# A four-layer convolution stack: transfers of layer 1 tied to its matmuls, layer 2's normalisation ahead of one copy of its column sums

## Chip, cores and metric

The kernel runs on one core of a Trainium2 chip, written in Bass and Tile. The metric is the device time of one execution in microseconds (us). Everything is float32.

## The reference

The input is x, four images of 16 channels of 512 x 512. Four layers each normalise their input in groups of two channels, apply a convolution and add the result to the input. Layers 1 and 2 are the ones concerned here.

```python
# layer 0: two blocks of three dilated 5x5 convolutions over neighbouring channels, tanh
x = x + L0(_gn(x))
# layer 1: quantise, 3x3 convolution of 16 to 16 channels, scale back
x_q = round(clip(x_cl / scale_input, -n, n))          # x_cl is _gn(x), scale_input from its largest magnitude
acc = conv(x_q, w_hwio, padding=1)
x = x + acc * (scale_input * scale_weight) + bias
# layer 2: a mean over 17 columns and then 17 rows, per channel
x = x + conv(conv(_gn(x), kx), ky)
# layer 3: a 3x3 complex convolution of the spectrum (rfftn, irfftn)
x = x + L3(_gn(x))
```

## The kernel before

The layers run one after the other, each from a tensor in HBM to the next (x1, x2, x3). `run` calls `layer0`, `layer1`, `layer2` and `layer3`. In the inner loops of all layers the order of the work is written out by hand (`tc.manual_schedule()`): each engine does its instructions in the order of the program text, and the SP engine (SyncE) issues loads and stores in that order too. A load that waits for its buffer holds up whatever SP has behind it.

**Layer 1** (`layer1`, lines 825 to 973) walks over 64 chunks of eight image rows; all four images are in a chunk together, each on its own 32 partitions (two rows by 16 channels). For chunk u:

- `load(u)` brings four transfers of 256 KB, one for each image b, from x1 into a tile `l1x` (line 890). The pool of these tiles has four buffers. Line 883 loads the row ahead of the first chunk, line 892 the last row.
- `rounded(u)` normalises and rounds it on ScalarE (ACT, line 900) and VectorE (DVE, lines 901 and 902) into one of three `l1q` tiles.
- `products(u)` issues 256 matmuls of 32 x 32 x 512 (line 915) into one of two PSUM tiles `l1p`: eight groups (n, which is a tap row a and a column shift d) by four images b by four output row pairs j. Each has a weight load of its own. The groups with d < 3 read `l1q`; the last two, d = 3, read the unrounded `l1x` and add the input.
- `write(u)` scales the result on ACT (line 929) into a tile `l1o` of three buffers, takes its statistics on DVE (line 931), and SP stores it in four transfers of 256 KB to x2 (line 933).

The order in one turn of the loop is load(u+2), products(u), rounded(u+1), write(u-1). After the loop, line 955 aggregates the statistics, and a chain of small operations gives layer 2's normalisation.

**Layer 0** already has the device that the change brings to layer 1: its `products` keeps the last matmul of each group in `marks`, and its `load` (line 200) makes a transfer wait for one of them by `add_manual_dep`, so many bytes to a mark.

**Layer 2** (`layer2`, lines 976 to 1092) walks over 64 images of one channel, i. `load(i)` (line 1011) brings 1 MB; `normal(i)` (line 1017) normalises on ACT into `l2n`; `first(i)` does the first pass, 32 matmuls with the band matrix (helper `box`, line 999), four ACT copies from PSUM into `l2y` (line 1028); `second(i)` does the second pass, 32 matmuls, and adds the input on DVE (line 1039), takes statistics (line 1040) and stores 1 MB to x3 (line 1041); `column_sums(i)` multiplies the result by three column vectors (line 1051), copies the sums on ACT into `l2s` (line 1056) and stores them on SP (line 1058). The product of each quarter hb of the image's rows leaves three rows of PSUM at partitions 32 hb to 32 hb + 2, and there is one ACT copy for each. Layer 3's edge products read these sums from HBM.

The order in one turn is load(i+3), first(i+1), column_sums(i-1), second(i), normal(i+2).

Of the kernel before, what the change touches and what calls it, by code (L numbers as in the profile page):

```python
# [744 lines left out]
class Kernel:  # L745
# [79 lines left out]
    def layer1(self, x1, x2, gn):  # L825
        tc, nc = self.tc, self.nc
        scale, bias, amax = gn
        with ExitStack() as ctx:
            wpool = ctx.enter_context(tc.tile_pool(name="l1w", bufs=1))
            xin = ctx.enter_context(tc.tile_pool(name="l1x", bufs=4))  # L830
            work = ctx.enter_context(tc.tile_pool(name="l1work", bufs=2))

            wrep = self.load(wpool, "l1_w")
# [38 lines left out]
            qs = [wpool.tile([P, 4, W + 2], F32, name=f"l1q_{i}") for i in range(3)]  # L872
            for q in qs:
                nc.vector.memset(q, 0.0)
            raws = {}

            def load(u):

                x = raws[u] = xin.tile([P, 4, W], F32, name=f"l1x_{u}", tag="x")
                if u < 0:  # L880
                    nc.vector.memset(x[:, 3], 0.0)
                    for b in range(B):
                        nc.sync.dma_start(x[32 * b + C : 32 * b + 32, 3], x1[b, 0])
                    return
                whole = 4 if u + 1 < NYB else 3
                if whole == 3:
                    nc.vector.memset(x[:, 3], 0.0)
                for b in range(B):
                    rows = x1[b, 8 * u + 1 : 8 * u + 1 + 2 * whole].rearrange("(k y) c w -> (y c) k w", y=2)
                    nc.sync.dma_start(x[32 * b : 32 * b + 32, 0:whole], rows)  # L890
                    if whole == 3:
                        nc.sync.dma_start(x[32 * b : 32 * b + C, 3], x1[b, H - 1])

            def rounded(u):
                lo = 3 if u < 0 else 0
# [11 lines left out]

            def products(u):
                ps = psum.tile([P, B, W], F32, name=f"l1p_{u}", tag="ps")
                for n, (a, d) in enumerate((a, d) for d in range(4) for a in range(2)):  # L910
                    for b in range(B):
                        for j in range(4):
                            v, k = (u - 1, 3) if a + j == 0 else (u, a + j - 1)
                            rows = slice(32 * b, 32 * b + 32)
                            nc.tensor.matmul(  # L915
                                ps[32 * j : 32 * j + 32, b, :],
                                wt[rows, a, d],
                                qs[v % 3][rows, k, d : d + W] if d < 3 else raws[v][rows, k],
                                start=(n == 0),
                                stop=(n == 7),  # L920
                                skip_group_check=True,
                            )
                raws.pop(u - 1)
                return ps

            def write(u, ps):
                o = work.tile([P, B, W], F32, name=f"l1o_{u}", tag="o", bufs=3)
                for k in range(0, B, 2):
                    nc.scalar.activation(o[:, k : k + 2], ps[:, k : k + 2], AF.Identity, bias=wbi, scale=osc)
                for b in range(B):  # L930
                    nc.vector.bn_stats(st[b][:, u, :], o[:, b, :])
                    dst = x2[b].rearrange("h c w -> (h c) w")
                    nc.sync.dma_start(dst[u * P : (u + 1) * P, :], o[:, b, :])

            with tc.tile_pool(name="l1ps", bufs=2, space=PSUM) as psum, tc.manual_schedule():
                for u in range(-1, 2):
                    load(u)
                for u in range(-1, 1):
                    rounded(u)
                last = None  # L940
                for u in range(NYB):
                    if u + 2 < NYB:
                        load(u + 2)
                    ps = products(u)
                    if u + 1 < NYB:
                        rounded(u + 1)
                    if last is not None:
                        write(u - 1, last)
                    last = ps
                write(NYB - 1, last)  # L950

            gps = ctx.enter_context(tc.tile_pool(name="l1gps", bufs=2, space=PSUM))
            mv = wpool.tile([P, B, 2], F32, name="l1mv")
# [22 lines left out]
    def layer2(self, x2, x3, sums, gn, l3):  # L976
        tc, nc = self.tc, self.nc
        res, under_way = [], []
        with ExitStack() as ctx:
# [3 lines left out]
            edge = ctx.enter_context(tc.tile_pool(name="l2edge", bufs=1))  # L983
            ps1 = ctx.enter_context(tc.tile_pool(name="l2p1", bufs=2, space=PSUM))
            ps2 = ctx.enter_context(tc.tile_pool(name="l2p2", bufs=2, space=PSUM))
            ps3 = ctx.enter_context(tc.tile_pool(name="l2p3", bufs=1, space=PSUM))
            gps = ctx.enter_context(tc.tile_pool(name="l2gps", bufs=1, space=PSUM))
            eps = [ctx.enter_context(tc.tile_pool(name=f"l2e{n}", bufs=1, space=PSUM)) for n in "us"]
            band = self.load(wpool, "c_band")
            cs = self.load(wpool, "c_cs")  # L990
            mv = wpool.tile([P, B, G, 2], F32, name="mv3")
# [21 lines left out]
            def normal(i):  # L1013
                b, c = divmod(i, C)
                g = c // 2
                xns[i] = work.tile([P, 4, W], F32, name=f"l2n_{i}", tag="xn")
                nc.scalar.activation(  # L1017
                    xns[i], xts[i], AF.Identity, bias=gn[b][1][:, g : g + 1], scale=gn[b][0][:, g : g + 1]
                )
# [25 lines left out]
            def column_sums(i):  # L1045

                b, c = divmod(i, C)
                o = outs.pop(i)
                pc = ps3.tile([P, W], F32, name=f"l2p3_{i}", tag="pc")
                for hb in range(4):  # L1050
                    nc.tensor.matmul(  # L1051
                        pc[32 * hb : 32 * hb + 3], cs[:, hb, :], o[:, hb, :], start=True, stop=True, skip_group_check=True
                    )
                so = work.tile([P, W], F32, name=f"l2s_{i}", tag="so")
                for hb in range(4):
                    nc.scalar.copy(so[32 * hb : 32 * hb + 3], pc[32 * hb : 32 * hb + 3])  # L1056
                for t in range(3):
                    nc.sync.dma_start(sums[b][t, c], so[t : t + 97 : 32])

# [9 lines left out]
            with tc.manual_schedule():  # L1069
                for i in range(3):  # L1070
                    load(i)
                normal(0)
                first(0)
                normal(1)
                for i in range(n + 1):
                    if i + 3 < n:
                        load(i + 3)
                    if i + 1 < n:
                        first(i + 1)
                    if i > 0:  # L1080
                        column_sums(i - 1)
                    if i < n:
                        second(i)
                    if i + 2 < n:
                        normal(i + 2)
                    advance()
                    if i > 0 and i % C == 0:
                        b = i // C - 1
                        res.append(self.group_stats(gps, self.stats, f"x3_{b}", mv[:, b], G))
                        if b == 1:  # L1090
                            under_way.append(self.edges(l3, 0, res, sums, tiles, *eps))
# [536 lines left out]
```

## Time and profile before

| what | value |
|---|---|
| median of three runs | 5569.73 us (5559.56 to 5571.75) |
| the profiled execution | 5572.08 us, its span 5570.3 us |
| granted TensorE clock | 0.978 |
| layer 1, first to last matmul's start (L915) | 3216.8 to 3860.2 us |
| layer 2, first pass to last column sum's start (L999, L1051) | 3890.5 to 4554.6 us |
| TensorE busy / DVE / ACT | 92% / 73% / 47% of the span |

The span runs from the first to the last instruction of the profiled execution. PE is TensorE's matmuls, PEld its weight loads, which overlap with them. A group of the page is read as: line, engine, operation, out<-in, partitions x elements, xcount | busy us, mean ns of one | idle time just before them, and what ended most of it; "issue" there is idle time in which the engine waited for nothing that the profile shows. A row of the timeline is read as: start in us, duration in us, engine, line, operation, tiles, xcount, and in brackets the idle time ahead of it and what ended it. A row of the windows gives a stretch, its length, the busy time of each engine with its instructions, the granted clock, the mean busy share of the 16 DMA engines and what they moved in GB/s.

### The profile page before, as it was taken

The page shows a single profiled execution, that of the slowest core. Times are in us where ns is not written, and L with a number is a line of the kernel's source. Part 1 is how long each engine was busy: PE and PEld are TensorE (multiplying, and loading weights), DVE is VectorE, ACT ScalarE, POOL GpSimd, SP SyncE. Part 2 cuts the span into 40 slices and gives each one's busy share as a digit, 9 for nine tenths or more (in the row PEclk, how much of TensorE's full clock was granted, in tenths as well). Part 3 has the DMA queues.
Part 4 walks back from the last instruction along what each step waited for, and adds up shares of the span by engine and source line. Part 5 has one row for each costly group of instructions (what it writes and reads, how often), then busy time and mean ns, then how long its engine had stood idle before and what let it go on. Part 6 is the DMA issues. An engine that isn't in the chain of part 4 may idle for free.

```text
span 5570.3 us, 267073 instructions
## 1 busy us (share of the span) xinstructions
PE 5105.7 (92%) x125040; PEld 3556.9 (64%) x125040; DVE 4044.1 (73%) x4738; ACT 2611.6 (47%) x4143; POOL 6.1 (0%) x18
## 2 busy tenths in 40 slices
PE   3999999999999989989999788887999979999999
PEld 2665665666675656666666545554887866777776
DVE  7766889657987659897678854445555568888887
ACT  2533335433345523443122444443665656666665
POOL 0000000000000000000000000000000000000000
PEclk9999999999999999999999999998999999999999
DMA  5555545565445555544454377876565655555554
GB/s 192 136 147 129 153 139 153 142 150 137 122 151 160 142 131 143 150 124 118 89 132 126 117 198 209 214 209 191 199 214 192 214 176 137 143 145 149 148 144 119
DMA packets 373827, 860.92 MB, mean 155 GB/s; under 512 B 52209, under 2 KB 74353, under 8 KB 356081
## 3 DMA queue, kind: packets, MB, share of 16 engines
q1 hardware_dynamic: 317072, 694.76, 44.1%
q10 hardware_dynamic: 55648, 149.08, 9.4%
q8 instruction: 979, 16.04, 1.3%
q14 instruction: 128, 1.04, 0.1%
HBM read 503.74 MB, written 339.90 MB: 151 GB/s over the span
## 4 chain that ended last, share of the span: by engine, by line
PE 84%; issue 5%; ACT 4%; DVE 4%; DMA 2%; SPq 1%; ACTq 0%; DVEq 0%
PE m L499 50%; PE l1p L915 10%; PE l2p L999 5%; PE u L1464 4%; PE s L1405 4%; PE u L1405 4%; PE u L1427 2%; PE pt L1439 2%; ACT l2n L1017 2%; ACT l2s L1056 2%; PE l2p L1051 1%; SPq L200 1%; DVE frame L415 1%; DMA frame<-y 0%; PE pr L1449 0%
## 5 line engine op out<-in xcount | busy, mean ns | idle before, releaser
L499 PE MATMUL m<-frame,l0w 32*32 32x512 f32 x86016 | 2920.8, 608 | 257.1 <-issue 151.7
L499 PEld LDWEIGHTS m<-frame,l0w 32*32 32x32 f32 x86016 | 1968.4, 104 | 1208.6 <-issue 604.0
L415 DVE SCALAR_TENSOR_TENSOR frame<-frame,frame 128x2376 f32<-128x2376 f32 x232 | 606.6, 2625 | 4.7 <-PE m L499 0.4
L915 PE MATMUL l1p<-l1q,l_wt 32*32 32x512 f32 x12288 | 489.2, 603 | 109.6 <-issue 68.1
L915 PEld LDWEIGHTS l1p<-l1q,l_wt 32*32 32x32 f32 x12288 | 274.4, 103 | 266.0 <-issue 186.0
L1039 DVE TENSOR_TENSOR l2o<-l2x,l2p 128x512 f32<-128x512 f32 x256 | 172.6, 674 | 283.1 <-PE l2p L999 283.1
L617 ACT ACTIVATE junk<-xb,neg 128x1024 f32<-128x1024 f32 x256 | 294.1, 1149 | 80.1 <-DVE top L601 38.2
L532 ACT COPY C<-m 128x1024 f32<-128x1024 f32 x64 | 61.6, 1014 | 537.2 <-PE m L499 408.7
L999 PE MATMUL l2p<-k_c_band,l2n 128*128 128x144 f32 (+1 forms) x2048 | 275.1, 295 | 36.5 <-DMA l2x<-x 15.5
L999 PEld LDWEIGHTS l2p<-k_c_band,l2y 128*128 128x128 f32 x2048 | 256.8, 190 | 75.0 <-issue 54.3
L999 PEld LDWEIGHTS l2p<-k_c_band,l2n 128*128 128x128 f32 x2048 | 262.2, 197 | 48.6 <-ACT l2n L1017 41.4
L999 PE MATMUL l2p<-k_c_band,l2y 128*128 128x144 f32 (+1 forms) x2048 | 284.3, 292 | 6.0
L901 DVE TENSOR_SCALAR l1t<-l1t 128x2048 f32<-128x2048 f32 x64 | 78.5, 1226 | 271.2 <-ACT l1t L900 271.2
L900 ACT ACTIVATE l1t<-l1x,l1own,l1own 128x1024 f32<-128x1024 f32 x128 | 151.8, 1233 | 237.4 <-DMA l1x<-x 234.6
L1464 PE MATMUL u<-k_c_hil,zt 128*128 128x128 f32 x2048 | 256.0, 279 | 0.0
L384 DVE STREAM_TRANSPOSE frame<-xp 128x1056 f32<-128x1056 f32 x128 | 161.6, 1278 | 127.0 <-ACT xp L358 127.0
L1464 PEld LDWEIGHTS u<-k_c_hil,zt 128*128 128x128 f32 x2048 | 238.5, 192 | 2.1 <-issue 0.8
L1440 ACT COPY zt<-pt 128x512 f32<-128x512 f32 x256 | 131.5, 601 | 210.3 <-PE pt L1439 210.3
L1028 ACT COPY l2y<-l2p 128x512 f32<-128x512 f32 x256 | 149.7, 585 | 169.1 <-PE l2p L999 169.1
L1370 DVE TENSOR_TENSOR xc<-l3n,k_c_tab 128x2048 f32<-128x2048 f32 x64 | 146.7, 2292 | 109.6 <-ACT l3n L1354 109.6
L915 PE MATMUL l1p<-l1x,l_wt 32*32 32x512 f32 x4088 | 213.3, 632 | 0.0
L1483 DVE SCALAR_TENSOR_TENSOR l3o<-u,l3t 128x256 f32<-128x256 f32 x512 | 192.8, 430 | 23.4 <-ACT l3t L1475 21.0
(302 smaller groups left out, 6553.0 us busy)
## 6 DMA issues: line engine op xcount, KB each, us to landing
y<-y ACTq DMA_DIRECT2D x128, 528.0 KB
frame<-y SPq DMA_DIRECT2D x512, 132.0 KB
xb<-in_x SPq DMA_DIRECT2D x128, 512.0 KB
x<-xb ACTq DMA_DIRECT2D x128, 512.0 KB
x<-l1o SPq DMA_DIRECT2D x256, 256.0 KB
l2x<-x SPq DMA_DIRECT2D x64, 1024.0 KB
x<-l2o SPq DMA_DIRECT2D x64, 1024.0 KB
l3x<-x SPq DMA_DIRECT2D x256, 256.0 KB
```

Source lines behind the costliest of these rows:

```text
L384: nc.vector.transpose(v[:, :, 4 + h : 68 : 2], xp)
L415: self.nc.vector.scalar_tensor_tensor(o, x, f, y, ALU.mult, ALU.add)
L499: ins = nc.tensor.matmul(ps[PX * j : PX * j + PX, i, :].rearrange("p (k r) -> p k r", r=64), w[rows, n], v[rows, k0 : k0 + 8, r0 : r0 + 64 ...
L617: nc.scalar.activation(junk, xs[h], f, bias=neg, accum_out=self.out_sums[n][:, 2 * t + h : 2 * t + h + 1])
L900: nc.scalar.activation(t[:, at], x[:, at], AF.Identity, bias=own[1], scale=own[0])
L915: nc.tensor.matmul(ps[32 * j : 32 * j + 32, b, :], wt[rows, a, d], qs[v % 3][rows, k, d : d + W] if d < 3 else raws[v][rows, k], start=(n ...
L999: nc.tensor.matmul(ps[:, lo:hi], lhs[:, k, at : at + P], band[:, j : j + hi - lo], start=(k == 0), stop=(k == 3), skip_group_check=True,)
L1028: nc.scalar.copy(yts[i][:, wb, :], ps)
L1039: nc.vector.tensor_add(o[:, hb, :], xt[:, hb, :], ps)
L1405: nc.tensor.matmul(ps[b][32 * j : 32 * j + 32], f[rows, n, j, :], x[rows, j, :], start=(i == 0), stop=(i == 2 and tag == "s"), skip_group_ ...
L1464: nc.tensor.matmul(po[:, bass.ts(k, P)], zt[:, b, k ^ 1, :], hil[:, k, :], start=False, stop=(k == 3), skip_group_check=True,)
L1483: nc.vector.scalar_tensor_tensor(o[:, v].rearrange("p k u -> p u k"), po[:, HW:W].rearrange("p (u k) -> p u k", u=2), s, t.rearrange("p (u ...
```

## The change

In layer 1 the input tiles get a fifth buffer and the output tiles a fourth. `products` keeps the last matmul of each of its eight groups in `marks`. A new helper `move` issues a transfer on SP and makes it wait for a mark: the load of image b for mark 2b, the store of image b for mark 2b + 1. Loads run three chunks ahead instead of two, and the stores of chunk u - 2 are issued in turn u, alternating with the loads; before, those of chunk u - 1 were issued right after its statistics. The first chunks' loads, ahead of the loop, have no marks to wait for.

In layer 2 the PSUM tile of the column sums is allocated once and cleared once, and one ACT copy of all 128 partitions takes the place of the four copies of three partitions. `normal(i + 2)` moves ahead of `column_sums(i - 1)`, so that ACT does it before that copy.

```diff
--- before.py
+++ after.py
@@ -827,7 +827,7 @@
         scale, bias, amax = gn
         with ExitStack() as ctx:
             wpool = ctx.enter_context(tc.tile_pool(name="l1w", bufs=1))
-            xin = ctx.enter_context(tc.tile_pool(name="l1x", bufs=4))
+            xin = ctx.enter_context(tc.tile_pool(name="l1x", bufs=5))
             work = ctx.enter_context(tc.tile_pool(name="l1work", bufs=2))
 
             wrep = self.load(wpool, "l1_w")
@@ -872,24 +872,30 @@
             qs = [wpool.tile([P, 4, W + 2], F32, name=f"l1q_{i}") for i in range(3)]
             for q in qs:
                 nc.vector.memset(q, 0.0)
-            raws = {}
-
-            def load(u):
-
+            raws, outs, marks = {}, {}, []
+
+            def move(n, to, src):
+
+                ins = nc.sync.dma_start(to, src).ins
+                if marks:
+                    tc.add_manual_dep(ins, marks[n].name, AFTER, reason="transfers spread over the chunk")
+
+            def tile_of(u):
                 x = raws[u] = xin.tile([P, 4, W], F32, name=f"l1x_{u}", tag="x")
+                if u < 0 or u + 1 == NYB:
+                    nc.vector.memset(x[:, 3], 0.0)
+
+            def load(u, b):
+
+                x = raws[u]
                 if u < 0:
-                    nc.vector.memset(x[:, 3], 0.0)
-                    for b in range(B):
-                        nc.sync.dma_start(x[32 * b + C : 32 * b + 32, 3], x1[b, 0])
+                    nc.sync.dma_start(x[32 * b + C : 32 * b + 32, 3], x1[b, 0])
                     return
                 whole = 4 if u + 1 < NYB else 3
+                rows = x1[b, 8 * u + 1 : 8 * u + 1 + 2 * whole].rearrange("(k y) c w -> (y c) k w", y=2)
+                move(2 * b, x[32 * b : 32 * b + 32, 0:whole], rows)
                 if whole == 3:
-                    nc.vector.memset(x[:, 3], 0.0)
-                for b in range(B):
-                    rows = x1[b, 8 * u + 1 : 8 * u + 1 + 2 * whole].rearrange("(k y) c w -> (y c) k w", y=2)
-                    nc.sync.dma_start(x[32 * b : 32 * b + 32, 0:whole], rows)
-                    if whole == 3:
-                        nc.sync.dma_start(x[32 * b : 32 * b + C, 3], x1[b, H - 1])
+                    nc.sync.dma_start(x[32 * b : 32 * b + C, 3], x1[b, H - 1])
 
             def rounded(u):
                 lo = 3 if u < 0 else 0
@@ -907,12 +913,13 @@
 
             def products(u):
                 ps = psum.tile([P, B, W], F32, name=f"l1p_{u}", tag="ps")
+                marks.clear()
                 for n, (a, d) in enumerate((a, d) for d in range(4) for a in range(2)):
                     for b in range(B):
                         for j in range(4):
                             v, k = (u - 1, 3) if a + j == 0 else (u, a + j - 1)
                             rows = slice(32 * b, 32 * b + 32)
-                            nc.tensor.matmul(
+                            ins = nc.tensor.matmul(
                                 ps[32 * j : 32 * j + 32, b, :],
                                 wt[rows, a, d],
                                 qs[v % 3][rows, k, d : d + W] if d < 3 else raws[v][rows, k],
@@ -920,34 +927,44 @@
                                 stop=(n == 7),
                                 skip_group_check=True,
                             )
+                    marks.append(ins.ins)
                 raws.pop(u - 1)
                 return ps
 
             def write(u, ps):
-                o = work.tile([P, B, W], F32, name=f"l1o_{u}", tag="o", bufs=3)
+                o = outs[u] = work.tile([P, B, W], F32, name=f"l1o_{u}", tag="o", bufs=4)
                 for k in range(0, B, 2):
                     nc.scalar.activation(o[:, k : k + 2], ps[:, k : k + 2], AF.Identity, bias=wbi, scale=osc)
                 for b in range(B):
                     nc.vector.bn_stats(st[b][:, u, :], o[:, b, :])
-                    dst = x2[b].rearrange("h c w -> (h c) w")
-                    nc.sync.dma_start(dst[u * P : (u + 1) * P, :], o[:, b, :])
+
+            def store(u, b):
+                dst = x2[b].rearrange("h c w -> (h c) w")
+                move(2 * b + 1, dst[u * P : (u + 1) * P, :], outs[u][:, b, :])
 
             with tc.tile_pool(name="l1ps", bufs=2, space=PSUM) as psum, tc.manual_schedule():
-                for u in range(-1, 2):
-                    load(u)
+                for u in range(-1, 3):
+                    tile_of(u)
+                    for b in range(B):
+                        load(u, b)
                 for u in range(-1, 1):
                     rounded(u)
                 last = None
-                for u in range(NYB):
-                    if u + 2 < NYB:
-                        load(u + 2)
-                    ps = products(u)
+                for u in range(NYB + 2):
+                    if u < NYB:
+                        ps = products(u)
+                    if u + 3 < NYB:
+                        tile_of(u + 3)
+                    for b in range(B):
+                        if u + 3 < NYB:
+                            load(u + 3, b)
+                        if u >= 2:
+                            store(u - 2, b)
                     if u + 1 < NYB:
                         rounded(u + 1)
-                    if last is not None:
+                    if 0 < u <= NYB:
                         write(u - 1, last)
                     last = ps
-                write(NYB - 1, last)
 
             gps = ctx.enter_context(tc.tile_pool(name="l1gps", bufs=2, space=PSUM))
             mv = wpool.tile([P, B, 2], F32, name="l1mv")
@@ -983,9 +1000,10 @@
             edge = ctx.enter_context(tc.tile_pool(name="l2edge", bufs=1))
             ps1 = ctx.enter_context(tc.tile_pool(name="l2p1", bufs=2, space=PSUM))
             ps2 = ctx.enter_context(tc.tile_pool(name="l2p2", bufs=2, space=PSUM))
-            ps3 = ctx.enter_context(tc.tile_pool(name="l2p3", bufs=1, space=PSUM))
+            pc = ctx.enter_context(tc.tile_pool(name="l2p3", bufs=1, space=PSUM)).tile([P, W], F32, name="l2p3")
             gps = ctx.enter_context(tc.tile_pool(name="l2gps", bufs=1, space=PSUM))
             eps = [ctx.enter_context(tc.tile_pool(name=f"l2e{n}", bufs=1, space=PSUM)) for n in "us"]
+            nc.vector.memset(pc, 0.0)
             band = self.load(wpool, "c_band")
             cs = self.load(wpool, "c_cs")
             mv = wpool.tile([P, B, G, 2], F32, name="mv3")
@@ -1046,14 +1064,12 @@
 
                 b, c = divmod(i, C)
                 o = outs.pop(i)
-                pc = ps3.tile([P, W], F32, name=f"l2p3_{i}", tag="pc")
                 for hb in range(4):
                     nc.tensor.matmul(
                         pc[32 * hb : 32 * hb + 3], cs[:, hb, :], o[:, hb, :], start=True, stop=True, skip_group_check=True
                     )
                 so = work.tile([P, W], F32, name=f"l2s_{i}", tag="so")
-                for hb in range(4):
-                    nc.scalar.copy(so[32 * hb : 32 * hb + 3], pc[32 * hb : 32 * hb + 3])
+                nc.scalar.copy(so, pc)
                 for t in range(3):
                     nc.sync.dma_start(sums[b][t, c], so[t : t + 97 : 32])
 
@@ -1077,12 +1093,12 @@
                         load(i + 3)
                     if i + 1 < n:
                         first(i + 1)
+                    if i + 2 < n:
+                        normal(i + 2)
                     if i > 0:
                         column_sums(i - 1)
                     if i < n:
                         second(i)
-                    if i + 2 < n:
-                        normal(i + 2)
                     advance()
                     if i > 0 and i % C == 0:
                         b = i // C - 1
```

## Prediction

> **What bounds the kernel now.** I read the page's groups first, then the busy time by windows to find the two layers that the change touches, then the waits and the timeline inside them. TensorE is busy 92% of the 5570.3 us span. Layer 1 (line L915) runs from 3216.7 to about 3861 us and layer 2 (L999, L1051) from 3890 to 4556; nothing else is edited, so everything before 3207 and after about 4575 is taken as unchanged.
>
> The page, DMA queues and costliest groups:
>
> ```profile
> q8 instruction: 979, 16.04, 1.3%
> ...
> L499 PE MATMUL m<-frame,l0w 32*32 32x512 f32 x86016 | 2920.8, 608 | 257.1 <-issue 151.7
> ...
> L915 PE MATMUL l1p<-l1q,l_wt 32*32 32x512 f32 x12288 | 489.2, 603 | 109.6 <-issue 68.1
> ```
>
> L915 is idle 109.6 us, 68.1 of it on "issue", that is, on nothing the profile shows. 38.9 of the rest is the start of the layer. No tile, buffer or engine holds TensorE there. Two windows, the loaded part of the layer and its end (microseconds; then busy time of PE, PEld, DVE, ACT, POOL; granted clock, DMA share, GB/s):
>
> ```profile
> 3238.26:3830.76 592.50, 525.13 (x15074) 319.31 (x15075) 288.11 (x354) 275.57 (x238) 0.00 (x0) 0.98 0.78 212
> 3841.00:3857.68 16.68, 16.68 (x530) 12.78 (x522) 7.79 (x11) 6.97 (x6) 0.00 (x0) 1.00 0.42 156
> ```
>
> The first holds 59 chunks of 256 matmuls: 592.5/59 = 10.04 us each. The second holds the last two, with loads over: 16.68/2 = 8.34 us each, PE never idle. So a chunk loses 1.70 us. The timeline of weight loads shows where (start, us, ..., then idle time before):
>
> ```profile
> 3503.24 1.34 PEld L915 LDWEIGHTS l1p<-l1q,l_wt 32*32 32x32 f32 x50
> 3504.82 4.00 PEld L915 LDWEIGHTS l1p<-l1q,l_wt 32*32 32x32 f32 x128 [0.24 <-issue]
> 3510.75 0.15 PEld L915 LDWEIGHTS l1p<-l1q,l_wt 32*32 32x32 f32 x11 [1.94 <-issue]
> ```
>
> One hole per chunk, always ahead of its last quarter (the residual products). The instruction queue explains it: 16.04 MB in 979 packets is 16.4 KB a packet, and TensorE's 250,080 instructions (125,040 matmuls and as many weight loads) over 979 give 255 a packet. A chunk has 512, so two packets, one per 4.17 us of an unstalled chunk. The hole comes at every second boundary. The DMA in the same chunk:
>
> ```profile
> 3503.00:3504.00 1.00, 1.00 (x51) 0.68 (x34) 0.89 (x2) 0.00 (x0) 0.00 (x0) 1.00 0.00 0
> 3504.00:3509.25 5.25, 5.25 (x173) 3.63 (x156) 2.86 (x5) 2.30 (x2) 0.00 (x0) 1.00 1.01 218
> 3509.25:3511.75 2.50, 1.45 (x46) 0.55 (x34) 0.00 (x0) 0.72 (x1) 0.00 (x0) 1.00 0.98 367
> 3511.75:3513.75 2.00, 2.00 (x83) 1.33 (x66) 0.31 (x1) 1.66 (x2) 0.00 (x0) 1.00 0.10 35
> ```
>
> SP issues four loads at 3503.11 and four stores at 3505.48. The engines are then full for 7.75 us, the loads at 218 GB/s and the stores at 367, and nearly empty for 2. A page of instructions asked for at about 3505.4 (a quarter into the chunk[...]) arrives at 3510.75, 1.5 us after the loads have drained: 5.3 us against 4.17. The page asked for at 3510.75 meets the empty stretch and is in time. That reading is inferred; no view shows a page's transfer.
>
> Layer 2 is simpler. The timeline of one steady image:
>
> ```profile
> 4002.67 3.02 PEld L999 LDWEIGHTS l2p<-k_c_band,l2y 128*128 128x128 f32 x24 [0.86 <-issue]
> 4002.68 4.54 PE L999 MATMUL l2p<-k_c_band,l2y 128*128 128x136 f32 x32
> 4002.91 2.34 ACT L1056 COPY l2s<-l2p 3x512 f32<-3x512 f32 x4 [0.51 <-PE l2p L1051]
> 4005.27 1.55 SPq L1058 DMA_DIRECT2D sums<-l2s  x3
> 4005.27 2.10 ACT L1017 ACTIVATE l2n<-l2x,bias_x,scale_x 128x2048 f32<-128x2048 f32 x1
> 4007.42 0.65 PEld L999 LDWEIGHTS l2p<-k_c_band,l2n 128*128 128x128 f32 x5 [0.41 <-ACT l2n L1017]
> 4007.42 0.74 PE L999 MATMUL l2p<-k_c_band,l2n 128*128 128x136 f32 x4 [0.21 <-ACT l2n L1017]
> ```
>
> The period is 9.77 us. ACT makes the four column-sum copies before it normalises the next image, and the normalisation ends 0.05 us before TensorE resumes: TensorE waits for it in every image.
>
> [...] The load phase ran at 218, the 128-partition stores at 367. [...]
>
> **The change, part by part, layer 1.** Bytes, matmuls, activations and vector work per chunk stay. Each of the eight transfers now waits for one of eight groups of 32 matmuls, so one of 256 KB starts every 8.34/8 = 1.04 us. By the rates above a load takes 256 KB/218 = 1.20 us and a store 0.71 us; a pair takes 1.91 of its 2.08 us. The queue is thus busy 92% of a chunk but never holds more than about two transfers, where it held eight.
>
> A page then waits for at most one or two transfers. I size the rest by layer 0, whose transfers are already tied to matmuls: 151.7 us of "issue" over 86016/128 = 672 pages is 0.226 us a page. In layer 1 the same column (68.1/59 = 1.15 us) stands for 1.70 us lost, a factor of 1.47, so an estimate of 0.33 us a page and 0.66 a chunk. That is my choice; the ends are 0 (the last two chunks) and the loss of now at both pages, 3.40. New chunk: 8.34 + 0.66 = 9.00. Gain: 1.04 us x 61 chunks = **63 us**.
>
> The other edits of layer 1 cost nothing, and here is the cover. SP waits 256 times for matmuls; behind it in its queue stand only this layer's transfers, and an extra wait of SP took 17 ns. The load for chunk u+3 is issued during chunk u, its last at 6/8 of the chunk, and lands about 2.8 us later (0.9 us to the first bytes, as after 3503.11, the store ahead and its own time), a chunk ahead of the rounding (4.8 us of ACT and DVE) that needs it; this is what the fifth input buffer is for. Without it the load would wait for chunk u-1's tile. Stores are a chunk late, covered by the fourth output buffer. At the end eight stores instead of four follow the last product: 8 x 0.71 = 5.7 us from about 3861, done by 3870 with the issue; the first load that reads them is issued at 3881.9, behind the 7.1 us of statistics (L955) and the chain after it. After instruction fetch, what is late next is issue itself: 8.34 us.
>
> **Layer 2.** ACT loses three copies of 0.58 us per image; a copy of 128 partitions takes no longer than one of 3 (585 ns in L1028 against 576 in L1056), as both have 512 columns. The normalisation starts right after the last l2y copy, at about 4002.4 instead of 4005.27, and ends 2.9 us before TensorE wants it. Its input's load was issued 13 us before that (3989.46), and 2 MB at layer 2's rate of 210 GB/s, the store ahead included, takes 10 us; so it should still be there. The copy of the sums then ends at about 4005.1 against 4005.25, so the SP stores behind it don't move. The wait's worth: from second pass to next pass is 4.74 us here (4002.68 to 4007.42). Near the end of the layer, where no normalisation stands in between, TensorE went from a second pass to its next work in 4545.82 - 4541.35 = 4.47. The gain is 0.27 us an image; the wait columns bound it from 0.21 (PE) to 0.45 (PEld). Times 56 images: 15 us (12 to 25). At the end, the last copies (2.34 us, 4555.29 on) hold the sums that layer 3's edge loads need: 1.75 us more. Together **17 us**. The memset of the sums' bank is one DVE instruction (a like one at L887 took 0.49 us) while DVE waits for weights, 6.5 us idle; 0. What is late next: TensorE itself, whose second pass takes 4.54 against the first's 4.13, as it waits for DVE's l2o (0.30 a pass).
>
> Sum: 63 + 17 = 80 us off the profiled 5572.08 gives 5492; that execution lies 2.35 us above the median, so against 5569.73 **5490 us**.
>
> **Rivals.** (a) Both pages stall. For: the queue has no empty stretch any more, and it was the empty stretch that saved every second page. Against: the full queue held eight transfers, now two. Its price: if each page took 1.25 us too long (5.4 us, what the page in the burst took), a chunk is 8.34 + 2.50 = 10.84, a loss of 49 us, less 17: 5602, slower. It decides the sign from 0.85 us a page in layer 1, and for the whole kernel from about 1.0. (b) The transfers become the bound. For: 1.91 of 2.08 us, and single transfers may leave holes. If eight take 9.4 us, the gain is 0.64 x 61 = 39, plus 17: 5514. (c) Nothing changes in layer 1, because the hole isn't from the burst, or the waits leave the transfers bunched: 5553 by layer 2 alone. The regular match of hole and burst speaks against it.
>
> **Chances.** Forecast 0.66, (a) 0.08, (b) 0.17, (c) 0.09. The best case is a chunk of 8.34, 61 x 1.70 = 104, with 25 in layer 2: 5441. The range, 5448 to 5545, leaves out (a), most of (c) and the last of the best case. A difference of 0.2% (11 us) is about what a measurement can tell from none. Faster: the forecast, (b) and half of (c), 0.87; within 0.2%: 0.05; slower: (a), 0.08.
>
> **What would show it.** Right: layer 1's chunks at about 9.0 us, from 644 us to 580 for the layer; holes under "issue" shorter and at both page boundaries; DMA share even across a chunk, at 0.85 to 0.95. In layer 2 no wait for l2n at L1017, images at 9.5 us, one l2s copy of 0.58 us. Wrong: holes of over 0.85 us at both boundaries; TensorE or ACT waiting for l1x on the path; the layer 2 load arriving after the normalisation wants it.

## The result, and the profile after

| | before | changed |
|---|---|---|
| median of four runs each, us | 5569.27 (5559.56 to 5571.75) | 5499.39 (5485.31 to 5501.45) |
| ratio, 95% interval | | 0.9872 (0.9852 to 0.9893) |
| span of the profiled execution, us | 5570.3 | 5499.7 |
| layer 1, first to last matmul's start | 643.4 | 596.8 |
| layer 1, a chunk | 10.03 | 9.28 |
| layer 2, first pass to last column sum | 664.1 | 638.0 |
| up to layer 1 / after layer 2 | 3216.8 / 1015.7 | 3219.0 / 1015.1 |

The change takes 69.9 us off; 80 were forecast (5490). The spans give the places: 46.6 us in layer 1 (63 forecast), 26.1 us in layer 2 (15, and 1.75 at the tail), 0.6 after it; layer 0, which is not edited, took 2.3 more. A chunk is here and below the start of the last residual product less that of the first, divided by 63.

The page after, busy time, queues and costliest groups:

```profile
PE 5084.4 (92%) x125040; PEld 3551.0 (65%) x125040; DVE 4047.2 (74%) x4739; ACT 2488.6 (45%) x3951; POOL 6.1 (0%) x18
...
q8 instruction: 979, 16.04, 1.3%
...
L499 PE MATMUL m<-frame,l0w 32*32 32x512 f32 x86016 | 2926.0, 609 | 253.5 <-issue 148.2
...
L922 PE MATMUL l1p<-l1q,l_wt 32*32 32x512 f32 x12288 | 484.3, 600 | 75.4 <-DVE l1q L912 39.5
```

TensorE's instructions and their 979 pages are the same, layer 0's group (L499) too. In layer 1 (now L922) idle time falls from 109.6 to 75.4 us, and what ended most of it is no longer "issue" but the start of the layer, 39.5 us, which stays. The waits (total us, times, longest) give what is left under "issue", 32.6 us where it was 68.1:

```profile
PE l1p L922 <- issue: 32.6, 51, 1.3
```

The loaded part of the layer, as a window (length; busy time of PE, PEld, DVE, ACT, POOL; clock, DMA share, GB/s):

```profile
3242.00:3780.00 538.00, 504.96 (x14773) 296.01 (x14764) 283.31 (x346) 270.37 (x232) 0.00 (x0) 1.00 0.74 228
```

The DMA share was forecast at 0.85 to 0.95. It went down, from 0.78 to 0.74, while the rate rose from 212 to 228 GB/s: the same bytes took less DMA time. The timeline of weight loads shows the holes that remain:

```profile
3500.71 0.16 PEld L922 LDWEIGHTS l1p<-l1q,l_wt 32*32 32x32 f32 x12 [1.54 <-issue]
...
3509.96 0.16 PEld L922 LDWEIGHTS l1p<-l1q,l_wt 32*32 32x32 f32 x12 [1.41 <-issue]
...
3514.91 0.24 PEld L922 LDWEIGHTS l1p<-l1q,l_wt 32*32 32x32 f32 x32 [1.33 <-issue]
```

From 3500.71 to 3509.96 is a chunk; 3514.91 lies half a chunk on. A chunk has two page boundaries, and holes now come at either. Those over 0.6 us number 77 in the layer's 64 chunks with 99.0 us in all, against 71 with 130.1 us before. SP's timeline shows that the transfers do leave one by one:

```profile
3502.94 0.67 SPq L879 DMA_DIRECT2D l1x<-x  x1
3504.00 0.34 SPq L879 DMA_DIRECT2D x<-l1o  x1
3505.06 0.30 SPq L879 DMA_DIRECT2D l1x<-x  x1
3506.15 0.34 SPq L879 DMA_DIRECT2D x<-l1o  x1
```

They are 1.06 to 1.09 us apart (1.04 forecast); where TensorE has a hole in between, up to 1.95. A steady image of layer 2, from its timeline:

```profile
3939.99 3.93 PEld L1017 LDWEIGHTS l2p<-k_c_band,l2n 128*128 128x128 f32 x32
3940.11 4.02 PE L1017 MATMUL l2p<-k_c_band,l2n 128*128 128x136 f32 x32
...
3944.65 2.10 ACT L1035 ACTIVATE l2n<-l2x,bias_x,scale_x 128x2048 f32<-128x2048 f32 x1
...
3945.03 4.54 PE L1017 MATMUL l2p<-k_c_band,l2y 128*128 128x136 f32 x32
...
3946.64 0.57 ACT L1072 COPY l2s<-l2p 128x512 f32<-128x512 f32 x1
```

The normalisation ends at 3946.75, 2.65 us before the next first pass starts at 3949.40. One copy of 0.57 us follows it. No matmul waits for `l2n` in a steady image; before, 57 did (total us, times, longest):

```profile
PEld l2p L999 <- ACT l2n L1017: 41.4, 58, 15.6
PE l2p L999 <- ACT l2n L1017: 14.4, 57, 2.7
```

The image takes 9.30 us, where 9.77 was measured before and 9.5 forecast. Before, weight load and matmul of a first pass started together (4007.42); now the weight load starts 0.12 us ahead (3939.99, 3940.11).

### The profile page after: what moved, and what is told of

It reads as the page before. It is cut to its first block, busy times and chain, and to the rows that moved or that the text cites. A ratio compares the mean times of both kernels' runs of the same rounds, so it can differ in the third digit from the quotient of the medians.

```text
span 5499.7 us, 267188 instructions
## 1 busy us (share of the span) xinstructions
PE 5084.4 (92%) x125040; PEld 3551.0 (65%) x125040; DVE 4047.2 (74%) x4739; ACT 2488.6 (45%) x3951; POOL 6.1 (0%) x18
## 3 DMA queue, kind: packets, MB, share of 16 engines
q8 instruction: 979, 16.04, 1.3%
q14 instruction: 128, 1.05, 0.1%
## 4 chain that ended last, share of the span: by engine, by line
PE 88%; DVE 6%; issue 4%; DMA 2%; SPq 1%; ACT 0%; ACTq 0%; DVEq 0%
PE m L499 52%; PE l1p L922 10%; PE l2p L1017 7%; PE u L1480 4%; PE s L1421 4%; PE u L1421 4%; PE u L1443 2%; PE pt L1455 2%; DVE l2o L1057 2%; PE l2p L1068 1%; DVE st L1058 1%; DVE frame L415 0%; PE pr L1465 0%; DVE A L537 0%; DVE B L536 0%
## 5 line engine op out<-in xcount | busy, mean ns | idle before, releaser
L499 PE MATMUL m<-frame,l0w 32*32 32x512 f32 x86016 | 2926.0, 609 | 253.5 <-issue 148.2
L499 PEld LDWEIGHTS m<-frame,l0w 32*32 32x32 f32 x86016 | 1984.6, 103 | 1194.0 <-issue 591.3
L922 PE MATMUL l1p<-l1q,l_wt 32*32 32x512 f32 x12288 | 484.3, 600 | 75.4 <-DVE l1q L912 39.5
L922 PEld LDWEIGHTS l1p<-l1q,l_wt 32*32 32x32 f32 x12288 | 252.5, 103 | 252.1 <-issue 175.6
L1017 PEld LDWEIGHTS l2p<-k_c_band,l2n 128*128 128x128 f32 x2048 | 262.3, 197 | 26.1 <-ACT l2n L1035 18.6
L939 DVE BATCH_NORM_STATS2 l1st<-l1o 128x6 f32<-128x512 f32 x256 | 158.2, 681 | 160.6 <-ACT l1o L937 160.6
L937 ACT ACTIVATE l1o<-l1p,k_l_bias,l_osc 128x1024 f32<-128x1024 f32 x128 | 147.2, 1200 | 247.6 <-PE l1p L922 241.7
L532 ACT COPY A<-m 128x1024 f32<-128x1024 f32 x64 | 61.6, 1014 | 309.0 <-PE m L499 215.1
```

Source lines behind the costliest of these rows:

```text
L499: ins = nc.tensor.matmul(ps[PX * j : PX * j + PX, i, :].rearrange("p (k r) -> p k r", r=64), w[rows, n], v[rows, k0 : k0 + 8, r0 : r0 + 64 ...
L922: ins = nc.tensor.matmul(ps[32 * j : 32 * j + 32, b, :], wt[rows, a, d], qs[v % 3][rows, k, d : d + W] if d < 3 else raws[v][rows, k], sta ...
L1017: nc.tensor.matmul(ps[:, lo:hi], lhs[:, k, at : at + P], band[:, j : j + hi - lo], start=(k == 0), stop=(k == 3), skip_group_check=True,)
```

## The experiments

Every ratio is to the kernel before, run beside it. The same layer 1 in two kernels can differ by 0.2 us a chunk (9.28 in the changed kernel, 9.09 in l1_only; before's own 9.83 to 10.03), so smaller differences are not read. Layer 0, which only the two paired kernels edit, ended in these traces anywhere from 3190 to 3219 us. For layer 1 the chunk is therefore a better measure than the total.

| kernel | median us | ratio (95%) | chunk, layer 1 | layer 2 |
|---|---|---|---|---|
| l1_only | 5503.59 | 0.9917 (0.9901 to 0.9933) | 9.09 | 661.1 |
| l2_only | 5522.67 | 0.9953 (0.9936 to 0.9970) | 9.83 | 638.1 |
| l2_order | 5522.80 | 0.9955 (0.9937 to 0.9972) | 9.87 | 638.2 |
| l2_copy | 5517.88 | 0.9944 (0.9923 to 0.9965) | 9.89 | 638.5 |
| l1_once | 5411.69 | 0.9773 (0.9744 to 0.9802) | 8.15 | 635.8 |
| l1_nomarks | 5485.10 | 0.9906 (0.9880 to 0.9933) | 9.13 | 638.1 |
| l1_two | 5506.22 | 0.9941 (0.9924 to 0.9958) | 9.64 | 637.5 |
| l1_paired | 5468.24 | 0.9874 (0.9844 to 0.9903) | 9.16 | 635.5 |
| l1_grouped | 5540.17 | 0.9976 (0.9963 to 0.9989) | 9.97 | 636.0 |
| l1_short | 5364.46 | 0.9659 (0.9627 to 0.9691) | 7.58 | 637.6 |
| l1_paired_grouped | 5497.62 | 0.9901 (0.9876 to 0.9925) | 9.33 | 638.1 |
| l1_lean | 5479.55 | 0.9870 (0.9844 to 0.9896) | 9.16 | 637.5 |

**The two layers apart.** l1_only has the diff's hunks of `layer1`, l2_only those of `layer2`.

> Layer 1 as changed, layer 2 as before. If the two halves are independent: layer 1's chunks at 9.27 us as in the changed kernel, 46 us less than before, about 5524 us, and layer 2's images at 9.77 us again. Rival: part of layer 1's gain comes with layer 2 (a shift of the pages of instructions, say): a sum with the run of layer 2 alone that misses 70 us by more than 10.

> Layer 2 as changed, layer 1 as before: images at 9.30 us instead of 9.77, 26 us less than before, about 5544 us; the prediction had put this at 17 us (5553). Rival: as for layer 1 alone.

The two ratios multiply to 0.9870, where the change has 0.9872: the gains are apart and add up. l1_only's total fell by 45.6 us, close to the 46.6 of the span above.

**Layer 2, one edit at a time.** l2_order only moves the normalisation, with the four copies kept; l2_copy only makes one copy, with the order kept:

```diff
+                    if i + 2 < n:
+                        normal(i + 2)
                     if i > 0:
                         column_sums(i - 1)
                     if i < n:
                         second(i)
-                    if i + 2 < n:
-                        normal(i + 2)
```

```diff
-                for hb in range(4):
-                    nc.scalar.copy(so[32 * hb : 32 * hb + 3], pc[32 * hb : 32 * hb + 3])
+                nc.scalar.copy(so, pc)
```

(l2_copy also allocates and clears `pc` once, as the change does.)

> Before, with only the normalisation moved ahead of the column sums; the four copies stay. If TensorE waits for the normalisation alone, the order is enough: images at 9.30 us, 26 us less, about 5544; the stores of the sums are issued 1.7 us later and nobody notices. Rival: the four copies behind it now hold up the next image's copies from PSUM, so that both edits are needed: between 5550 and 5570.

> Before, with only the one copy of the sums for four; the normalisation stays behind it. The copy ends 1.76 us earlier and the normalisation with it, at about 4005.6 of the timeline of before, where TensorE wants it at about 4007: the copy alone is enough as well, images at 9.30 us, 26 us less, about 5544. Rival: only the order takes the wait away for good: 9.5 us or more, 5555 to 5570.

The layer takes 638.2 and 638.5 us, as with both edits: either takes the whole wait away, and the second then has nothing left to gain. The waits of l2_order (total us, times, longest):

```profile
PEld l2p L999 <- ACT l2n L1017: 19.0, 2, 16.1
PE l2p L999 <- ACT l2n L1017: 18.6, 2, 16.0
```

Two waits are left of 58, the longest at the start of the layer.

**Layer 1, are the loads the cause?** l1_once is the changed kernel with no loads after the first three chunks; their tiles are used again, so later chunks see other rows:

```diff
             def tile_of(u):
+                if u > 2:
+                    raws[u] = raws[u % 3]
+                    return
...
             def load(u, b):
                 x = raws[u]
+                if u > 2:
+                    return
```

> The changed kernel, but layer 1 loads only its first chunks and uses their three tiles again for all others, so its results are of those rows; stores, matmuls, ACT and DVE work as in the changed kernel. If the holes of TensorE are pages of instructions held up by the transfers onto 32 partitions: chunks of 8.34 to 8.5 us, some 50 us less than the changed kernel, about 5450. Rival, the holes are TensorE's own or any transfer makes them: chunks stay at 9.2, about 5499.

A window of it:

```profile
3240.00:3700.00 460.00, 460.00 (x14544) 440.89 (x14524) 278.67 (x339) 258.00 (x227) 0.00 (x0) 1.00 0.35 133
```

PE is never idle in these 460 us, though the stores and 114 instruction pages still run in them. A chunk takes 8.15 us; this is taken as TensorE's own pace, and the rest of 10.03 or 9.28 is lost when loads run too. No run keeps the loads and drops the stores, so this doesn't tell the loads from the mere amount of traffic (133 GB/s here, 228 in the changed kernel).

**Are the waits for the products the cause?** l1_nomarks leaves them out, so that all eight transfers of a chunk, load and store alternating, are issued together; l1_two makes two bunches of four:

```diff
                 ins = nc.sync.dma_start(to, src).ins
-                if marks:
-                    tc.add_manual_dep(ins, marks[n].name, AFTER, reason="transfers spread over the chunk")
```

```diff
-                    tc.add_manual_dep(ins, marks[n].name, AFTER, reason="transfers spread over the chunk")
+                    tc.add_manual_dep(ins, marks[4 * (n // 4)].name, AFTER, reason="transfers spread over the chunk")
```

> The changed kernel without the waits for the matmuls; five input and four output buffers, loads three chunks ahead, stores two behind. The transfers of a chunk then go out together as soon as the tile of chunk u - 2 is free. If the spreading makes layer 1's gain: chunks of about 10.0 us, 5545. Rival, the deeper buffers make it: 9.3, 5499.

> The changed kernel with two marks instead of eight: two loads and two stores at the first group of a chunk, two and two at the fifth. If a page is held up by the depth of the queue ahead of it: between before and changed, chunks of 9.4 to 9.7 us, 5508 to 5526. Rival, a page goes through only when the queue runs empty, which two bunches leave room for once per page: 8.6 to 9.0 us, 5460 to 5485.

By the chunk they are not: without any wait it takes 9.13 us. The total is less clear. Its ratio, 0.9906, is less of a gain than the change's 0.9872, and the intervals just overlap; l1_lean below, also without waits, has 0.9870. Two bunches, between the two in spread, take 9.64 us. That is the figure expected if the depth of the queue held up a page, but l1_nomarks, whose queue is deeper, speaks against the depth; the last part of this section comes back to it. A window of l1_nomarks, one chunk's transfers:

```profile
3512.00:3519.00 7.00, 7.00 (x231) 4.83 (x219) 4.56 (x6) 4.57 (x4) 0.00 (x0) 1.00 0.97 297
```

The bunch that took 7.75 us before takes 7.0, at a rate between the 218 and 367 GB/s of before's two phases.

**The order of loads and stores.** l1_grouped is l1_nomarks with the four loads issued first and the four stores after them, and no other edit:

```diff
-                    for b in range(B):
-                        if u + 3 < NYB:
+                    if u + 3 < NYB:
+                        for b in range(B):
                             load(u + 3, b)
-                        if u >= 2:
+                    if u >= 2:
+                        for b in range(B):
                             store(u - 2, b)
```

> The run without waits for matmuls, with the four loads of a chunk issued ahead of its four stores instead of in turn with them. A new theory, from the DMA shares: layer 1 is bound by the one DMA engine that also carries TensorE's pages of instructions; its data (7.70 us a chunk before, 6.6 to 6.75 where loads and stores alternate) and two pages of 1.2 us each fill a chunk (10.1 of 10.03 before, 9.2 of 9.1 without waits). Then the grouping takes the data back to 7.5 to 7.7 us and the chunk to 9.9 to 10.1. Rival, the deeper buffers and the earlier issue of the stores made the gain: 9.1 us as in the run without waits.

It gives all of layer 1's gain back: 9.97 us a chunk, against 9.13 with the order alternated. (By the totals' ratios, 0.9976 and 0.9906, the order is worth 39 us or 0.6 us a chunk, a little less.) TensorE's idle time under "issue" from 3238 to 3760 us, in before, l1_grouped and l1_nomarks:

```profile
PE l1p L915 <- issue: 58.5, 51, 2.2
PE l1p L920 <- issue: 58.1, 51, 2.4
PE l1p L920 <- issue: 26.8, 37, 1.6
```

The windows of l1_grouped, loads and then stores:

```profile
3512.75:3517.50 4.75, 4.75 (x165) 3.86 (x157) 2.47 (x4) 4.46 (x4) 0.00 (x0) 1.00 1.01 222
3517.50:3520.00 2.50, 1.82 (x55) 0.48 (x39) 2.26 (x2) 0.10 (x1) 0.00 (x0) 1.00 1.03 376
```

The two phases of before are back, and 7.25 us. The data queue's share of the loaded part (75.8%, against 72.9% in l1_nomarks) times the chunk gives 7.6 us of data a chunk grouped and 6.7 alternated: 0.9 us, beside the chunk's 0.84. Neither run has the waits, so whether waits without the alternation would have gained anything was not tried.

**Wide loads.** In the prediction's windows the loads, onto 32 partitions, run at 218 GB/s and the stores, from 128, at 367. To see whether the number of partitions makes the difference, l1_paired lays x1 out by pairs of rows, so that one load fills 128 partitions (layer 0's stores to x1 are re-aimed); l1_paired_grouped is the same without waits and with the loads ahead of the stores.

```diff
-                rows = x1[b, 8 * u + 1 : 8 * u + 1 + 2 * whole].rearrange("(k y) c w -> (y c) k w", y=2)
-                move(2 * b, x[32 * b : 32 * b + 32, 0:whole], rows)
+                if b < whole:
+                    move(2 * b, x[:, b], x1[4 * u + 1 + b].rearrange("b y c w -> (b y c) w"))
```

> The changed kernel with x1 laid out by row pairs, images inside, so that each of the four loads of a chunk fills all 128 partitions of a quarter of the tile instead of 32 partitions of all of it; same bytes, same number of transfers, the values as before. If the loads onto 32 partitions (218 GB/s) hold up the pages: loads near the stores' 370 to 400 GB/s, chunks of 8.4 to 8.8 us, 5447 to 5471. Rival, the bytes or the number of transfers hold them up, whatever the partitions: 9.2 us, 5499. Layer 0's stores into the new layout are also 512 KB on 128 partitions, so its time should not move.

> The run with x1 by row pairs, without waits for matmuls, the four loads (128 partitions each) ahead of the four stores. Layer 2's images move as many bytes by 128 partitions in 6.0 us of DMA time. If the one engine's load sets the chunk: about 6.0 + 2.4 = 8.4 us, some 45 us less than the changed kernel. Rival, the grouping itself costs, whatever the partitions: 9.5 us or more. In between (9.0 to 9.2): loads and stores one after the other are no quicker on 128 partitions than in turn.

Windows of l1_paired_grouped, a stretch of its loads and one of its stores:

```profile
3516.25:3517.50 1.25, 1.25 (x58) 0.94 (x38) 0.36 (x1) 1.25 (x2) 0.00 (x0) 1.00 1.02 377
3510.00:3512.25 2.25, 1.79 (x56) 0.72 (x28) 1.28 (x2) 0.90 (x1) 0.00 (x0) 1.00 1.05 398
```

Wide loads run at 377 GB/s, narrow ones (l1_grouped) at 222, or 0.59 of it. Grouped, that brings the chunk from 9.97 to 9.33. Alternated, with the waits of the change, it brings nothing that can be told from the noise (9.16, against 9.28 and 9.09 for the narrow loads of the changed kernel and of l1_only). Why not was not tried.

**One DMA engine for data and pages?** In most kernels the time of data in a chunk plus that of two pages (each about 1.2 us of packets by the instruction queue's share) came close to the chunk as a window of the layer has it: 9.16 of 9.14 us in l1_nomarks, 10.10 of 10.03 before. So I formed the theory that one engine carries all the pages and is full. l1_short is l1_nomarks with six of the eight groups of products, so that a chunk needs one and a half pages:

```diff
-                for n, (a, d) in enumerate((a, d) for d in range(4) for a in range(2)):
+                for n, (a, d) in enumerate((a, d) for d in (0, 2, 3) for a in range(2)):
...
-                                stop=(n == 7),
+                                stop=(n == 5),
```

> The run without waits for matmuls, with two of the eight groups of a chunk's matmuls left out (the column shift d = 1), so that its results lack these taps; 192 matmuls and 1.5 pages of instructions a chunk, TensorE's own issue 6.26 us, transfers as they were. If one DMA engine carries data and pages: 6.6 + 1.5 x 1.24 = 8.5 us a chunk. Rival, the pages are merely late (a page wanted every 4.17 us and held up behind the queue) and the engines otherwise have room: the data alone bound it, 6.7 to 7.2 us.

Its DMA queues in the layer (packets, MB, share of 16 engines):

```profile
q1 hardware_dynamic: 64436, 117.21, 87.7%
q8 instruction: 84, 1.38, 1.5%
```

A chunk takes 7.58 us. Were all pages on one engine, and the data even over the 16, that engine would have to be busy 87.7 + 16 x 1.5 = 112% of the time, and 8.5 us was expected. The theory falls, though not by a wide margin, as the share itself reads 105% in a short window above; so does its rival's figure, which was lower than 7.58. l1_paired_grouped speaks against it as well: 6.3 us of data and two pages give 8.7, and the chunk took 9.33.

**The buffers.** l1_lean is l1_nomarks with the buffers of before (four in, three out) and the loads two chunks ahead again:

```diff
-            xin = ctx.enter_context(tc.tile_pool(name="l1x", bufs=5))
+            xin = ctx.enter_context(tc.tile_pool(name="l1x", bufs=4))
...
-                o = outs[u] = work.tile([P, B, W], F32, name=f"l1o_{u}", tag="o", bufs=4)
+                o = outs[u] = work.tile([P, B, W], F32, name=f"l1o_{u}", tag="o", bufs=3)
...
-                    if u + 3 < NYB:
-                        tile_of(u + 3)
+                    if u + 2 < NYB:
+                        tile_of(u + 2)
```

> The run without waits for matmuls, with before's four input and three output buffers and loads two chunks ahead: against before, layer 1 only stores a chunk later and each store goes out behind a load. If the alternation of loads and stores is the whole of layer 1's gain: DMA data 6.7 us a chunk, chunks of 9.1 to 9.3 us, about 70 us less than before with layer 2's gain. Rival, the extra buffers are needed for it as well (a load that lands too late for its rounding, an output tile that comes free too late): chunks of 9.6 us or more, with ACT or TensorE waiting for l1x or l1o.

It is as fast as the changed kernel (0.9870, against 0.9872), with no waits and no buffer more than before. Its waits in the loaded part:

```profile
ACT l1t L904 <- DMA l1x<-x: 260.8, 57, 6.4
...
PE l1p L920 <- issue: 25.2, 34, 2.0
```

ACT waits for its load in nearly every chunk, and TensorE does not notice. With l1_grouped, which has the deeper buffers and no gain, this rules the buffers out as the cause. No kernel that computes the whole reference is clearly ahead of the change: l1_paired (0.9874) and l1_lean lie within its interval.

**When do the pages start?** The traces hold every packet of the instruction queue, 16.4 KB each (16.04 MB over 979), one to a page. At the 255 instructions a page that the prediction counts, a page is about 128 weight loads with their matmuls, so the boundaries can be counted. In l1_short, whose chunk has 192 weight loads, 57 of the 64 steps from one hole to the next (a hole is here a gap of over 0.6 us between the starts of two weight loads) are 127, 128 or 256 loads long: the holes belong to the pages, not to a place in the chunk. From one boundary to the next, exactly one page starts. In the chunk of before that the prediction reads, a boundary lies at 3504.82. The next page starts at 3508.13, while the loads still run, and lands at 3509.51, and TensorE goes on at 3510.75. The instruction queue from 3508.10 to 3509.60 (5.8% of 16 engines' 1.5 us is about 1.4 us):

```profile
q8 instruction: 1, 0.02, 5.8%
```

Layer 1 from 25 us after its first weight load to 45 us before its last, times in us:

| kernel | a chunk | a page starts after its boundary, mean | its packet takes, mean | pages with a hole after them |
|---|---|---|---|---|
| before | 10.03 | 2.29 | 1.25 | 65 of 113 |
| l1_grouped | 9.97 | 2.36 | 1.19 | 63 of 114 |
| l1_two | 9.64 | 2.27 | 1.18 | 108 of 112 |
| changed | 9.28 | 1.95 | 1.34 | 82 of 110 |
| l1_nomarks | 9.13 | 1.93 | 1.24 | 65 of 112 |

In all five, a hole ends a median 1.36 to 1.42 us after the page has landed. A page that comes too late is moved little more slowly (1.32 us against 1.14 for the others in before, 1.42 against 1.12 in the changed kernel); above all it starts late. In these kernels no page starts sooner than 1.05 us after its boundary. A page with a hole after it started a median 3.14 us after it in before and 3.20 in l1_grouped, 2.23 in l1_nomarks and 2.00 in the changed kernel. In l1_two nearly every page has its hole; that its two bunches a chunk each meet one of the two pages would explain this, but is an inference. In l1_short start, packet and landing to going on are 2.41 + 1.20 + 1.42 = 5.03 us a page, and 1.5 pages make 7.55 of its 7.58 us.

## Why the prediction was right and where it was not

**The sign and the size** held: 69.9 us of 80. In layer 1 that is in part luck: the chunk is as short without the waits that were forecast to bring the gain.

**Layer 2: right mechanism, a term too small.** The wait went away, TensorE's own passes are what is late now, and nothing else came. The term "4.74 against 4.47, 0.27 us an image" was mis-sized: the step from a second pass to the next first pass is now 4.37 us (3935.74 to 3940.11), and the first pass itself is 0.11 shorter (4.13 to 4.02), which fits its weight load's start 0.12 us ahead of the matmul. Together 0.48 us, times 56 images 26.9; 26.1 was measured. My reference of 4.47 ended at a column sum (L1051) and not at a first pass, so it was no floor for this step. Of the two bounds I named, PEld's idle time (0.45) was the good one: the wait held up the weight load as well as the matmul. The 1.75 us for the tail came out as 0.6 at most.

**Layer 1: the place and about the size right, the cause wrong.** Right: the loss is pages of instructions that come late beside the transfers; l1_once takes the loads away and the holes with them. Right too: what was costed at nothing. SP's waits, the late stores and the memset show nowhere, and ACT's wait for loads fell from 234.6 to 48.7 us. The step that failed is "a pair takes 1.91 of its 2.08 us. The queue is thus busy 92% of a chunk but never holds more than about two transfers", with "A page then waits for at most one or two transfers" drawn from it. It sums a load alone and a store alone, whatever their order, and makes the short queue the gain. Measured, the data queue is busy 72% of a chunk (6.7 us), and l1_nomarks, with eight transfers issued together, has a chunk no longer (9.13 against 9.28) and pages that start no later (1.93 us after the boundary against 1.95; 2.29 before). What pays is the alternation that the diff brought in along with the waits: l1_grouped and l1_nomarks differ in it alone, by 0.84 us a chunk. The terms: TensorE's own pace 8.15, not 8.34; a loss of (9.28 - 8.15) / 2 = 0.57 us a page on average, not 0.33; so 0.75 us a chunk gained, not 1.04. (The 68.1 us that went into the 0.33 are those of all 64 chunks, divided by 59; the 59 have 66.1, which moves the estimate by 0.01 only.)

**The rivals.** (a) was right that stalls come at both page boundaries, but at 0.57 us a page on average, short of the 0.85 from which it decides. (b) has a chunk of 9.4, nearer to the measured 9.28 than the forecast's 9.00, but it named a full queue, and the queue is less full than before. (c), no gain in layer 1, is ruled out by l1_only. One of its reasons, that the hole isn't from the burst, has something in it: l1_nomarks keeps the burst and has the shorter chunk.

**Open:** what holds back the start of a page, and on which engine. Beside loads and stores, pages with a hole after them start a median 3.14 us after the boundary in before and 2.00 in the changed kernel; l1_once, without the loads, has no hole from 3240 to 3700 us, but no run here shows how a transfer holds back a page. Nor is the data's time alone what counts: l1_paired_grouped has less of it (6.3 us) than l1_nomarks (6.7) and no shorter chunk (9.33 against 9.13).

## What to carry to other kernels

Where a DMA queue carries loads onto few partitions and stores, try to issue them in turn rather than all of one and then all of the other, and try the order alone before adding waits and buffers for it; here it was worth 0.84 us of a 9.97 us chunk. Where an edit does two things at once, as here order and waits, price them apart, since a good total can hide a wrong cause. If a wait holds up a weight load too, read its worth from PEld's idle time and not PE's: here 0.45 and 0.21 us an image, where 0.48 was gained. Where TensorE idles under "issue", count its instructions from hole to hole.

## What the runs showed of the hardware

Loads onto 32 partitions ran at 222 GB/s alone and stores from 128 at 376 (l1_grouped), and the two alternated at 297 over their 7.0 us (l1_nomarks). With no loads running, TensorE took a matmul and its weight load of 32 x 32 every 31.8 ns (8.15 us / 256) with no hole from 3240 to 3700 us (l1_once), its pages coming beside traffic of 133 GB/s and taking about 1.03 us each (1.6% of 16 engines' 460 us, over 114 pages); with all transfers and three quarters of the instructions (l1_short), the queues ran at 283 GB/s and a chunk took 7.58 us, and at that rate the pages still came one per 5.05 us (7.58 / 1.5). Beside loads and stores, in the five kernels of the last table, a page's packet took 1.18 to 1.34 us, and TensorE went on a median 1.36 to 1.42 us after it had landed.
